# A recurrent layer with interleaved input products: groups of two steps in place of three, and an aligned instruction stream on TensorE

## The chip, the cores and the metric

One core of a Trainium2 chip runs the kernel. The metric is the device time of one execution, in microseconds (us). For the kernel before there are nine executions, with a median of 3041.02 us (3037.76 to 3044.69). A difference below 0.2%, some 6 us, is about what a measurement of this kernel can't tell from no change.

## What is computed

There are N = 64 sequences of T = 256 steps with D = 1024 features. Layer 0 is a plain recurrent network whose result is added to its input; layer 1 scales by a gate that doesn't depend on the step:

```python
xW = jnp.einsum('ntd,dh->nth', x, Wx) + b
next_h = jnp.tanh(prev_h @ Wh + xw)          # 256 times, one after the other
x = x + h_t
h = jax.nn.silu(q_pool @ W1.T + b1)
gate = jax.nn.sigmoid(h @ W2.T + b2)
# Haar levels of v, each times gate, put together again; then x + (v + that)
```

A Haar transform that is multiplied by one gate at all levels and undone is a multiplication by that gate, so layer 1 is a factor of 2 + gate for each sequence and feature. All in float32.

## The kernel before, in words

Two kinds of work take turns on TensorE.

**Steps of h.** `h @ Wh` for one step is done by Strassen's method: seven products (`strassen_product`, L192) in place of eight. A product is 16 calls of `nc.tensor.matmul` (L197), each 32 rows by 128 columns on a quarter of the array. Plain float32 takes two passes, so that each call becomes two weight loads and two matmuls on the chip: 64 instructions a product, 448 a step, 224 of them matmuls. The order in a step is product 1, 4, 2, 5, 6, 7, 3, so that what the next step needs first is ready first; `tanh` (L756), the transposes (L760) and the additions (L780 to L806) run on ScalarE and VectorE beside the next products. The input part `xw` of a step reaches the accumulators by a copy on ScalarE before the products (`put_part`, L611 to L614).

**Pairs of x.** `x @ Wx` is computed for a pair of two steps at once (`S = 2`), in three parts for precision, by `XWork.whole` (L333): 48 matmuls of 128x512 (L276) in a one-pass format, each with one weight load, 96 instructions. They go to the banks `mixed` and `main`. ScalarE takes `mixed` (L321), GpSimd adds the bias (L322), VectorE adds `main` (L376), and the sum goes to DRAM (`store`, L384) and comes back in the layout of the steps (`reload`, L388, eight DMAs).

The first 12 steps (0 to 11, `ALONE = 12`) are handled by another loop (L508), with half a pair beside each step. From step 12 on the loop at L743 runs **groups** of steps; the order on every engine and on SP, which issues the transfers, is the program's own (the schedule is manual). `groups` (L632) holds their lengths: 80 groups of `M = 3`, and 4 steps at the end. After each group `beside_x` (L654) fills the gap with pairs of x: it stores the sum of the pair that was computed last (`later`), not before `mark`, the copy of product 6 in the last step (L794), loads the x of a later pair (`load_next`), issues the reload, and computes the pair `coming` with `now.whole()` (L666). If that pair is needed within the next group, it is stored and reloaded at once, and a second pair follows in the same gap (`many`, L665, L701 to L704). Since a group of three takes one and a half pairs, gaps of one pair and of two alternate. In the gap VectorE adds h to x for the last step (`residual`), GpSimd multiplies by the factor (`scale`), finished pairs are stored to y (`store_done`), ScalarE puts the first accumulators of the next group (after `take_mixed`), and `kept_step` handles an early step that had been set aside, one action a gap.

The sum of a pair, its split parts (`x1`, `x2`) and the high bits have one buffer each; the tiles `xw` have four in turn; the x of pairs has six.

## Time and profile before

| what | value |
|---|---|
| median of nine executions | 3041.02 us |
| the profiled execution's own time | 3044.69 us |
| its span, first to last instruction | 3042.8 us |
| outside the span | 1.9 us |
| VectorE, ScalarE, GpSimd busy | 59%, 28%, 25% |
| data queue, share of 16 DMA engines | 28.1% |
| granted TensorE clock | 1.00 |

The profiled execution is the slowest of the nine. The page gives busy time by engine, the chain of work that ended last, and groups of equal instructions; matmuls are pipelined and their ends are modelled, so that TensorE counts as busy for nearly all of the span whether or not it is fed at its best rate. What it really takes is read from the start of one stretch to the start of the next. "issue" is time for which the profile shows no other engine or transfer as the cause. The trace records the start of every weight load and matmul, of the semaphore waits on the engine's sequencer, and of every DMA packet, those that bring instructions among them.

### The profile page before, as it was taken

What the parts mean: (1) busy time and instruction counts of PE and PEld (TensorE: products, weight loads), DVE (VectorE), ACT (ScalarE), POOL (GpSimd) and SP (SyncE); (2) the same over time, 40 slices, a digit from 0 to 9 for tenths busy, and PEclk for the clock granted to TensorE, in tenths of its full rate; (3) what the DMA queues carried; (4) which work ended last, traced back from release to release, by engine and by line L of the source; (5) the groups of instructions that cost most, each with busy time, mean ns of one, the idle gap of its engine ahead of it and who ended that gap; (6) DMA issues with size and microseconds to landing.
All of it is one profiled execution on the core that took longest, in us unless ns stands there. A gap on an engine that the chain in (4) does not pass through costs nothing.

```text
span 3042.8 us, 141755 instructions
## 1 busy us (share of the span) xinstructions
PE 3030.9 (100%) x63862; PEld 2716.0 (89%) x63862; DVE 1802.2 (59%) x4928; ACT 863.6 (28%) x2641; POOL 775.1 (25%) x521
## 2 busy tenths in 40 slices
PE   9999999999999999999999999999999999999999
PEld 6888999988889998999988889989899988888998
DVE  7555555655556656556655555556555655555555
ACT  3222222222222222222222223222222222222222
POOL 2223222232222222222222222222222222222221
PEclk9999999999999999999999999999999999999999
DMA  7323222333322222222222322222222222322222
GB/s 264 119 100 103 93 93 93 109 103 104 111 94 86 86 97 94 93 86 86 93 99 99 104 89 86 86 86 100 98 86 86 86 100 99 107 92 86 86 86 83
DMA packets 164605, 300.40 MB, mean 99 GB/s; under 512 B 44192, under 2 KB 110496, under 8 KB 164000
## 3 DMA queue, kind: packets, MB, share of 16 engines
q1 hardware_dynamic: 163856, 290.81, 28.1%
q8 instruction: 501, 8.21, 1.1%
q14 instruction: 104, 0.85, 0.1%
q10 hardware_dynamic: 144, 0.52, 0.1%
HBM read 154.93 MB, written 136.31 MB: 96 GB/s over the span
## 4 chain that ended last, share of the span: by engine, by line
PE 98%; DMA 1%; POOL 0%; issue 0%; DVE 0%; SPq 0%; DVEq 0%; ACT 0%
PE main L276 30%; PE acc L197 22%; PE mixed L276 16%; PE m_h L197 14%; PE main_h L197 14%; PE m L197 1%; DMA wh<-wh 0%; DMA h0T<-condT 0%; DMA w<-w1T 0%; PE gate_ps L214 0%; POOL sum L322 0%; DMA x<-xT 0%; DMA b_row<-b 0%; DVE x L300 0%; SPq L132 0%
## 5 line engine op out<-in xcount | busy, mean ns | idle before, releaser
L276 PE MATMUL main<-wx,x 128*128 128x512 f32 x4064 | 945.8, 389 | 0.2 <-DVE x L300 0.2
L276 PEld LDWEIGHTS main<-wx,x 128*128 128x128 f32 x4064 | 762.1, 188 | 161.0 <-issue 2.6
L501 POOL TENSOR_TENSOR x<-x,factor 128x512 f32<-128x512 f32 x242 | 312.4, 1291 | 1316.6 <-DVE x L619 933.3
L322 POOL TENSOR_TENSOR sum<-sum,b_row 128x512 f32<-128x512 f32 x254 | 423.5, 1677 | 835.0 <-ACT sum L321 783.6
L276 PE MATMUL mixed<-wx,x 128*128 128x512 f32 x2032 | 494.0, 395 | 0.0
L276 PEld LDWEIGHTS mixed<-wx,x 128*128 128x128 f32 x2032 | 374.9, 188 | 92.1 <-issue 16.9
L756 ACT ACTIVATE h<-h 128x128 f32<-128x128 f32 x976 | 275.7, 306 | 561.2 <-DVE h L780 373.8
L300 DVE TENSOR_TENSOR x<-x,x_high 128x1024 fp32r<-128x1024 f32 x127 | 180.5, 1421 | 261.6 <-PE main L276 261.6
L760 DVE STREAM_TRANSPOSE hT<-h 128x128 f32<-128x128 f32 x972 | 297.8, 306 | 38.3 <-ACT h L756 38.2
L376 DVE SCALAR_TENSOR_TENSOR sum<-main,sum 128x512 f32<-128x512 f32 x254 | 175.4, 691 | 199.6 <-PE main L276 175.7
L197 PE MATMUL acc<-wh,s 128*32 128x128 f32 x8160 | 278.7, 273 | 1.0 <-issue 0.9
L197 PE MATMUL acc<-t,hT 128*32 128x128 f32 x8160 | 273.1, 273 | 2.3 <-issue 2.2
L197 PE MATMUL acc<-wh,hT 128*32 128x128 f32 x8160 | 273.9, 273 | 0.5 <-issue 0.5
L197 PE MATMUL m_h<-t,s 128*32 128x128 f32 x7808 | 266.2, 273 | 0.5 <-issue 0.3
L197 PE MATMUL main_h<-wh,s 128*32 128x128 f32 x7808 | 265.7, 273 | 0.6 <-issue 0.5
L197 PE MATMUL main_h<-t,s 128*32 128x128 f32 x7808 | 264.2, 273 | 0.2
L197 PE MATMUL m_h<-wh,hT 128*32 128x128 f32 x7808 | 262.1, 274 | 0.1
L305 DVE SCALAR_TENSOR_TENSOR x<-x_high,x 128x1024 fp32r<-128x1024 f32 x127 | 182.6, 1438 | 132.4 <-PE mixed L276 132.3
L321 ACT ACTIVATE sum<-mixed 128x512 f32<-128x512 f32 x254 | 146.9, 598 | 362.9 <-DMA sum_d<-sum 192.5
L197 PEld LDWEIGHTS m_h<-wh,hT 128*32 128x32 f32 x7808 | 213.0, 110 | 29.4 <-issue 29.2
L197 PEld LDWEIGHTS acc<-wh,s 128*32 128x32 f32 x8160 | 234.7, 110 | 3.1 <-issue 3.1
L197 PEld LDWEIGHTS acc<-wh,hT 128*32 128x32 f32 x8160 | 230.8, 110 | 3.2 <-issue 1.8
(81 smaller groups left out, 2740.2 us busy)
## 6 DMA issues: line engine op xcount, KB each, us to landing
x<-xT SPq DMA_DIRECT2D x127, 512.0 KB, 4.6
sum_d<-sum SPq DMA_DIRECT2D x127, 512.0 KB, 2.9
xw<-sum_d SPq DMA_DIRECT2D x1016, 64.0 KB, 2.0
yT<-x SPq DMA_DIRECT2D x122, 512.0 KB, 2.8
wh<-wh SPq DMA_DIRECT2D x8, 512.0 KB, 10.8
w<-w1T SPq DMA_DIRECT2D x8, 512.0 KB, 8.5
w<-w2T SPq DMA_DIRECT2D x8, 512.0 KB, 4.3
wx<-wx SPq DMA_DIRECT2D x7, 512.0 KB, 8.6
```

The lines of the kernel that those rows point to most:

```text
L197: nc.tensor.matmul(out=out[q * R : (q + 1) * R], lhsT=a[:, k * R : (k + 1) * R], rhs=wh_s.sides[i][k][:, q], start=first and k == 0, stop= ...
L276: nc.tensor.matmul(out=acc[h], lhsT=v[:, k * P : (k + 1) * P], rhs=wx_s[k][which][:, h * HALF : (h + 1) * HALF], start=start and k == 0, s ...
L300: nc.vector.tensor_sub(self.x1, x, self.high)
L305: nc.vector.scalar_tensor_tensor(out=self.x2, in0=self.high, scalar=1.0 + DOWN, in1=pairs[i], op0=ALU.mult, op1=ALU.subtract)
L321: nc.scalar.activation(s, self.mixed[h], AF.Copy, scale=-1.0)
L322: nc.gpsimd.tensor_add(s, s, b_row[:, h * HALF : (h + 1) * HALF])
L376: nc.vector.scalar_tensor_tensor(out=v, in0=self.main[h], scalar=1.0 + DOWN, in1=v, op0=ALU.mult, op1=ALU.add)
L501: nc.gpsimd.tensor_mul(of_step(x, s), of_step(x, s), blocks(factor))
L756: nc.scalar.activation(quad(h, j), quad(h, j), AF.Tanh)
L760: nc.vector.transpose(quad(hT, j), quad(h, j))
```

## The change

`M` becomes 2. `groups` becomes 120 groups of two steps and 4 steps at the end. A group of two needs one pair, so that the test for a second pair is never met: each of the 121 gaps (one ahead of the first group, and one after each group of two) holds one pair. The pair that a group needs is the one computed in the gap before the last, and it is stored and reloaded in the gap just ahead of the group.

In each pair, ahead of the last two matmuls (`h == 1 and k == B - 2`), `nc.tensor.addr_align(256)` is issued, when `whole` is not followed by a second pair. The built program holds 121 such instructions, with an alignment of 256 instructions, no offset, and up to 255 no-ops as filler.

```diff
-M = 3
+M = 2
...
+BLOCK = 256
...
-        def whole(self) -> None:
+        def whole(self, aligned: bool = False) -> None:
...
             for h in range(2):
                 for k in range(B):
+                    if aligned and h == 1 and k == B - 2:
+                        nc.tensor.addr_align(BLOCK)
                     x_matmul(self.main, self.x0, 0, h, k, stop=True)
...
-    groups = [M] * ((T - ALONE) // M - 1) + [(T - ALONE) % M + M]
+    groups = [M] * ((T - ALONE) // M - 2) + [(T - ALONE) % M + 2 * M]
...
-        now.whole()
+        now.whole(not many)
```

The built programs have as many instructions on VectorE, ScalarE, GpSimd and the DMA queues as before; on TensorE's sequencer there are 631 semaphore waits in place of 671.

## The prediction

> **What bounds the kernel now.** I read the page first: who is busy, and whose chain ends last.

> ```profile
> span 3042.8 us, 141755 instructions
> PE 3030.9 (100%) x63862; PEld 2716.0 (89%) x63862; DVE 1802.2 (59%) x4928; ACT 863.6 (28%) x2641; POOL 775.1 (25%) x521
> ...
> q8 instruction: 501, 8.21, 1.1%
> ...
> PE 98%; DMA 1%; POOL 0%; issue 0%; DVE 0%; SPq 0%; DVEq 0%; ACT 0%
> ```

> TensorE's stream is the chain; nothing else is near. But "busy" hides slow feeding, so the second view is the chain of waits over one gap of two pairs and the group behind it (start us, us, what):

> ```profile
> 957.72 3.85 PE mixed L276 x16
> 961.57 7.25 PE main L276 x32
> 968.82 3.63 PE mixed L276 x16
> 972.45 7.25 PE main L276 x32
> 979.70 1.01 PE m_h L197 x32
> 980.71 1.75 PE acc L197 x64
> ```

> A pair behind steps of h takes 3.85 + 7.25 us, a pair behind a pair 3.63 + 7.25: entering x costs 0.22 us. The first product of h after x takes 1.01 us where two products take 1.75: returning costs 0.14 us. The third view is the sums over whole stretches (us, busy by engine): a clean group of three, a gap of one pair, a gap of two, and another group of three.

> ```profile
> 909.59:928.07 18.48, 18.48 (x673) 18.28 (x673) 11.64 (x44) 6.73 (x24) 2.59 (x2) 1.00 0.04 15
> 928.07:939.17 11.10, 11.10 (x52) 8.93 (x49) 6.58 (x13) 2.17 (x7) 4.77 (x3) 1.00 0.52 173
> 957.65:979.63 21.98, 21.98 (x100) 17.95 (x97) 11.71 (x18) 4.31 (x10) 8.11 (x5) 1.00 0.54 184
> 626.48:646.58 20.10, 19.41 (x673) 18.40 (x673) 11.94 (x44) 6.82 (x24) 2.69 (x3) 1.00 0.10 34
> ```

> The same 672 matmuls took 18.48 us once and 20.10 us another time. The chain inside the slow group says where:

> ```profile
> 640.32 1.74 PE acc L197 x62
> 642.06 0.23 issue
> 642.28 0.30 PE acc L197
> ...
> 645.31 0.67 PE acc L197 x26
> 645.98 0.27 issue
> 646.24 0.41 PE acc L197 x3
> ```

> These are breaks that no engine or data transfer ended. From the starts of all matmuls in the trace, 39 of the 80 groups of three take 18.477 us to within 1 ns, and the other 41 lose between 0.02 and 1.63 us: 16.0 us in all. I numbered TensorE's instructions in program order (two weight loads and two matmuls for a plain float32 call, one of each for x, and the semaphore waits). In most of these groups the first late matmul, 0.1 us or more behind a clean group's, stands at 193 to 195 modulo 256. Row q8 gives the reason: 501 packets of 8.21 MB, 16,384 bytes each, for TensorE's 128,398 records, so 256 instructions a packet. The stalls are **instruction blocks that arrive late**. They are almost all in the third step: no group has lost anything at the end of its first step, the sum is 1.2 us at the end of the second and 16.0 us at the end of the third. Leaving x, the sequencer is well ahead of the array (a matmul of x takes 227 ns, one of h 27.3); in h that lead is used up, and nothing rebuilds it before the next gap.

> [...]

> **The change part by part.** The sum is made in the profiled execution (3044.69 us, span 3042.8).

> *Transitions.* A clean group of three is 18.477 us. Its third step, start to start, is 6.113, so a clean group of two is 12.364. A gap of one pair is 11.108 (mean of 41, from 11.101 to 11.146); gaps of two average 21.987.
> Before: 80 x 18.477 + 455.4 (41 gaps of one) + 879.5 (40 gaps of two) = 2813.1, and 16.0 of stalls: 2829.1 us.
> After: 120 x 12.364 + 121 x 11.108 = 2827.8 us, without stalls.
> So 40 more round trips between h and x cost **+14.7 us**. Nothing hides them: they are the array's own stream, and their size does not vary with the stalls or with the length of the gap ahead.

> *Stalls taken away.* **-16.0 us**, since there is no third step. What remains is the stall of first and second steps. From below it is zero. From above, by the mean of all 80 groups at the end of the second step, 1.2 us / 80 x 120 = 1.8 us. The alignment decides where in that interval: it starts a block four instructions ahead of h, so blocks end near matmuls 126, 254 and 382 of a group's 448. Fifteen groups of before have boundaries within some 10 matmuls of these places, and together they lost 0.04 us in two steps: 0.3 us for 120. I take **+0.4 us**. The third boundary also lies ahead of the mark (behind product 6 of the second step, matmul 384), from which the pair's store starts, so data traffic does not meet that fetch at its start.

> *The no-ops.* A cycle has 2 x 448 + 96 + 5 semaphore waits = 997 instructions, so 27 no-ops fill it to 1024, four blocks. No row shows a no-op. The nearest rows are the sequencer's own semaphore waits, 51 ns each in the trace: 27 x 51 = 1.4 us a gap. The cover is the queue of x matmuls: the stream had lost nothing at the end of any first step, so the sequencer enters h with a full lead, which it can only have gained during x. Below: nothing. Above: 120 x 1.4 = 165 us, bare. The 40 semaphore waits that go could give 2 us if they were bare, and they are as well covered. I take 0 for both.

> *Work that moves to a shorter gap.* Every gap now has what only the two-pair gaps had: the reload must land and ScalarE must put the first accumulators before h resumes, in 11.1 us and not 22.

> ```profile
> 956.33 0.34 SPq L386 DMA_DIRECT2D sum_d<-sum  x1
> 956.76 0.39 SPq L119 DMA_DIRECT2D x<-xT  x1
> 961.19 3.62 SPq L399 DMA_DIRECT2D xw<-sum_d  x8
> ```

> ```profile
> 964.56 0.67 ACT L614 COPY acc<-xw 128x128 f32<-128x128 f32 x3 [2.21 <-DMA xw<-sum_d]
> ```

> This gap began at 957.65. The store leaves ahead of it, the reload waits on SP for the store's landing, and the put ends at 965.2, 7.6 us in. Over all 40 gaps of two the last put ends 2.1 to 7.8 us in. So 3.3 us remain of 11.1 at worst: cost 0, and beyond that 1 us per us and gap. Behind the reload on SP stands only the y store; behind the put on ScalarE only the copy for h. DVE is busy 6.6 of 11.1 us in a gap of one, GpSimd 4.8. One store, one load, eight reloads and one y store a pair are the same counts as before; the queued early steps (one action a gap) only finish sooner.

> *The end.* The last four steps exist in both. Before, they hold 2.4 us of stalls, with the last pair's store and two y stores beside them. The same transfers stand there after; I take the same, between 0 and twice that.

> **Sum**: +14.7 - 16.0 + 0.4 = **-0.9 us**, 3044.69 - 0.9 = 3043.8 us in terms of the profiled execution. That one is the slowest of nine, 3.67 us above the median. The stalls are the part of the chain that varies from one group to the next with no change of work. If the median execution simply has 3.67 us less of them, the change takes less away from it, and its own time stays at 3043.8. If the difference lies elsewhere, it becomes 3041.02 - 0.9 = 3040.1. I hold the first for twice as likely and forecast **3042.5 us**: no change that can be told. Own range 3038 to 3047.

> **The rivals.**

> *The no-ops are not covered (slower).* If they pass through the array's queue at the rate of h (27.3 ns for two instructions), 27 x 13.65 = 0.37 us x 120 = 44 us, 3087 us; bare on the sequencer 165 us, 3209 us. It decides from the point at which the sequencer is less than 1.4 us ahead when it meets them. For: no no-op is in the trace. Against: 227 ns a matmul in x leaves the sequencer idle most of the time. Chance 0.08.

> *The stalls come back (slower).* The fixed places may suit badly, for instance because each short gap leaves fetches behind data traffic (DMA share 0.52 in a gap, 0.04 in a clean group). At the 0.2 us that a group of three lost on average: 24 us, 3067 us. Against: fifteen groups with the same places. Chance 0.07, with smaller forms of it inside the forecast's range.

> *The alignment does nothing.* Then the mean over all places holds, 1.8 us of stalls in place of 0.4: 3043.9 us from the forecast, within its range. It is part of its chance.

> *Transitions shrink (faster).* If entering x is slow because the sequencer arrives late from the third step, groups of two would save 0.23 us in each of 121 gaps, 28 us: 3015 us. Against: gaps behind stalled and clean groups take the same 11.10 us. Chance 0.10, with partial gains.

> **How the numbers follow.** Forecast 0.75, slower rivals 0.15, faster 0.10. The range, 3036 to 3050, is the forecast's own with a few us towards partial forms of the rivals on both sides.

> **What would show it.** Groups of two at 12.36 us nearly without exception; 121 gaps near 11.11 us; about 514 instruction packets (27 x 120 more instructions); puts ending before 8 us in a gap; the mean step unchanged at 6.11. It would be wrong if gaps took over 11.2 us (no-ops or late puts), if groups lost more than 0.05 us on average, or if gaps fell under 11 us.

## The result, and the profile after

The changed kernel takes **3056.13 us** (median of nine, 3054.71 to 3057.66), the kernel before 3040.37 (29 executions, 3034.79 to 3045.45). The ratio is 1.0051, with a 95% interval of 1.0043 to 1.0060: slower by half a per cent, where no change was forecast. The profiled execution took 3057.18 us.

The page answers the questions of the prediction's first view:

```profile
span 3055.4 us, 144905 instructions
PE 3035.7 (99%) x63862; PEld 2708.7 (89%) x63862; DVE 1799.0 (59%) x4928; ACT 871.1 (29%) x2641; POOL 843.7 (28%) x521
...
q8 instruction: 514, 8.42, 1.1%
...
PE 98%; DMA 1%; issue 0%; POOL 0%; DVE 0%; SPq 0%; DVEq 0%; ACT 0%
```

TensorE is still the chain, there are 13 more instruction blocks as counted, but its busy share is 99% and no longer 100%. The waits of TensorE (line waited for: us in total, times, longest) say that this is one break; the second row had 3.6 us in ten waits before:

```profile
PE main L277 <- issue: 10.1, 1, 10.1
PE acc L198 <- issue: 2.7, 4, 1.1
```

10.1 us, once. The chain shows where (start us, us, what): in the very first gap, ahead of the last two matmuls of the pair, which is where the alignment stands.

```profile
186.54 6.80 PE main L277 x30
193.34 10.11 issue
203.45 1.19 PE main L277 x2
204.65 1.86 PE m_h L198 x32
206.51 2.48 PE acc L198 x64
```

The products of h behind it also take 1.86 and 2.48 us in place of 1.01 and 1.75. The sums over stretches show why. The first column is the length in us; then follow the busy time of TensorE, its weight loads, VectorE, ScalarE and GpSimd, the granted clock, the DMA share and GB/s. In order: the first gap, a later gap, the first group, and the time from 197.63 us on for which the clock was lowered.

```profile
182.58:204.58 22.00, 11.89 (x53) 9.06 (x49) 7.62 (x11) 3.26 (x7) 6.34 (x3) 0.84 0.12 40
429.73:440.83 11.10, 11.10 (x52) 8.93 (x48) 6.59 (x13) 2.27 (x7) 5.16 (x3) 1.00 0.57 173
204.58:218.52 13.94, 13.94 (x449) 13.44 (x449) 7.18 (x27) 4.45 (x15) 1.28 (x1) 0.88 0.05 17
...
197.63:207.87 10.24, 4.42 (x66) 3.50 (x70) 0.69 (x1) 1.21 (x2) 0.00 (x0) 0.50 0.01 2
```

Later gaps take 11.10 us, and later groups 12.36 by the starts of their matmuls, as forecast. The first gap takes 22.00: 10.9 too many. From 197.63 us, inside its break, the clock is at one half for 10.24 us; the last 4.4 of them lie behind the break and make the first group 1.58 us longer. Together 12.5 us.

What stands in that break is on record too: line 346, the alignment, has its own entry among the sources (engine, operation, count, duration of one, first and last start).

```profile
L346 PEldq NOP  x3437: 13/13/13, 189.1 to 3020.6; - x191
```

3437 no-ops are 120 x 27 + **197**. The trace has 197 in the first gap, from 189.12 to 203.38 us, 73 ns apart (14.3 us), though each record lasts only 13. In every other gap there are 27, over 1.9 us. What stands ahead of the first alignment is the whole first part of the program and no cycle of 997 instructions, so its filler is whatever is left to the next block. The late matmuls of the kernel before stood at 193 to 195 modulo 256 by my count, so I take it that some 62 instructions are loaded ahead of the kernel's own. With them, the count of TensorE's instructions to that place is 59 modulo 256, and 256 - 59 = 197. (The runs below that work out their offsets from this 59 got the number of no-ops that they asked for, 37 in their first gap.) The no-ops begin 4.06 us before the array is through with the matmuls queued ahead of them, there as in each of the other 120 gaps; the other 10.2 us are the break.

### The profile page after: what moved, and what is told of

It is laid out like the page before. It is cut to its first block, busy times and chain, and to the rows that moved or that the text cites. A ratio compares the mean times of both kernels' runs of the same rounds, so it can differ in the third digit from the quotient of the medians.

```text
span 3055.4 us, 144905 instructions
## 1 busy us (share of the span) xinstructions
PE 3035.7 (99%) x63862; PEld 2708.7 (89%) x63862; DVE 1799.0 (59%) x4928; ACT 871.1 (29%) x2641; POOL 843.7 (28%) x521
## 3 DMA queue, kind: packets, MB, share of 16 engines
q1 hardware_dynamic: 163856, 290.81, 27.3%
## 4 chain that ended last, share of the span: by engine, by line
PE 98%; DMA 1%; issue 0%; POOL 0%; DVE 0%; SPq 0%; DVEq 0%; ACT 0%
PE main L277 30%; PE acc L198 22%; PE mixed L277 16%; PE m_h L198 15%; PE main_h L198 14%; PE m L198 1%; DMA h0T<-condT 0%; DMA wh<-wh 0%; DMA w<-w1T 0%; PE gate_ps L215 0%; POOL sum L323 0%; DMA x<-xT 0%; DMA b_row<-b 0%; DVE x L301 0%; SPq L133 0%
## 5 line engine op out<-in xcount | busy, mean ns | idle before, releaser
L277 PE MATMUL main<-wx,x 128*128 128x512 f32 x4064 | 946.5, 389 | 10.3 <-issue 10.1
L504 POOL TENSOR_TENSOR x<-x,factor 128x512 f32<-128x512 f32 x242 | 358.6, 1482 | 2042.4 <-issue 1177.1
L277 PEld LDWEIGHTS main<-wx,x 128*128 128x128 f32 x4064 | 762.3, 188 | 171.4 <-issue 12.7
L323 POOL TENSOR_TENSOR sum<-sum,b_row 128x512 f32<-128x512 f32 x254 | 447.2, 1781 | 50.6 <-DMA w<-w1T 43.8
L301 DVE TENSOR_TENSOR x<-x,x_high 128x1024 fp32r<-128x1024 f32 x127 | 171.1, 1347 | 253.5 <-PE main L277 253.5
L777 ACT COPY y<-m_h 128x128 f32<-128x128 f32 x244 | 65.0, 266 | 779.1 <-PE m_h L198 763.9
L198 PE MATMUL acc<-wh,s 128*32 128x128 f32 x8160 | 271.4, 273 | 0.4 <-issue 0.4
L198 PE MATMUL m_h<-t,s 128*32 128x128 f32 x7808 | 259.6, 273 | 0.0
L198 PE MATMUL main_h<-wh,s 128*32 128x128 f32 x7808 | 259.5, 273 | 0.0
L306 DVE SCALAR_TENSOR_TENSOR x<-x_high,x 128x1024 fp32r<-128x1024 f32 x127 | 191.9, 1511 | 86.9 <-PE mixed L277 86.8
L783 DVE TENSOR_TENSOR h<-acc,y 128x128 f32<-128x128 f32 x244 | 71.2, 292 | 280.8 <-PE acc L198 280.8
```

What stands on the lines that cost most here:

```text
L198: nc.tensor.matmul(out=out[q * R : (q + 1) * R], lhsT=a[:, k * R : (k + 1) * R], rhs=wh_s.sides[i][k][:, q], start=first and k == 0, stop= ...
L277: nc.tensor.matmul(out=acc[h], lhsT=v[:, k * P : (k + 1) * P], rhs=wx_s[k][which][:, h * HALF : (h + 1) * HALF], start=start and k == 0, s ...
L301: nc.vector.tensor_sub(self.x1, x, self.high)
L306: nc.vector.scalar_tensor_tensor(out=self.x2, in0=self.high, scalar=1.0 + DOWN, in1=pairs[i], op0=ALU.mult, op1=ALU.subtract)
L323: nc.gpsimd.tensor_add(s, s, b_row[:, h * HALF : (h + 1) * HALF])
L504: nc.gpsimd.tensor_mul(of_step(x, s), of_step(x, s), blocks(factor))
```

## The experiments

Theory A: the first alignment's no-ops made the loss, and 53 or so are free. Rivals: the first gap, now of one pair, was too short for its work; the no-ops or the transitions cost something everywhere; the lost time in groups is chance. Each run was measured beside the kernel before, whose median went from 3038.56 to 3041.11 us between them, so that ratios are the better measure between runs. "The groups lose" always means: in the run's one profiled execution, against clean groups of 18.477 us (three steps), 12.364 (two) or 24.590 (four).

**The first filler spread over 17 gaps.**

```diff
+STEPS = [96 + 10 * g for g in range(16)]
...
-                        nc.tensor.addr_align(BLOCK)
+                        nc.tensor.addr_align(BLOCK, offset=STEPS.pop(0) if STEPS else 0)
```

> The changed kernel, but with the 197 no-ops of its first alignment spread: the first 17 gaps get 37 no-ops each, by offsets that grow by 10 a gap, and end at the same block positions; the other gaps keep 27. Theory A (the first alignment meets an instruction position that needs 197 no-ops, at 73 ns each 14.3 us, of which some 4.0 are covered by queued matmuls; then the clock is halved for 10.2 us): the 10.3 us break, 0.7 us in the last two matmuls and 1.6 us in the first group go, and the median falls by 12 to 13 us, to 3042.5 to 3045. The first gap takes 11.1 us. Theory B (the first gap is slow because the work of that gap, now of one pair and not of two, is late: a transfer or an engine): the gap stays at 20 us or more, and the time at 3056. Theory C (transitions cost more than the trace says, and the first gap is a side show): the time falls by less than 6 us.

Measured: 3045.52 us, 10.6 below the changed kernel; against the kernel before, 1.0024 (1.0014 to 1.0033). No gap in its trace is over 11.15 us, the longest group is 12.64, and the chain at the same place has no break:

```profile
184.56 7.25 PE main L278 x32
191.81 1.01 PE m_h L199 x32
192.82 1.75 PE acc L199 x64
```

Theory A holds. The two profiled executions differ by 12.7 us, as expected. The medians fall by less than the 12 to 13 us expected: 10.6 us, or some 8 by the ratios (1.0051 and 1.0024). More on that below. Theory B falls: the same gap with the same work takes 11.1 us.

**Groups of two without alignment.**

```diff
-        now.whole(not many)
+        now.whole()
```

> Groups of two without any alignment. Theory A: no no-ops, so no break in the first gap, 121 gaps of 11.10 to 11.15 us; stalls of 1 to 4 us in the groups of two, since blocks end anywhere; the median at 3043 to 3047, that is 0.1 to 0.2% above the kernel before, and 9 to 13 us below the changed one. Theory B (a gap of one pair at the start is too short for its work): the first gap stays at about 22 us and the time near 3056. If alignment matters as much as the change supposes, this one is slower than the spread alignment by more than 2 us; I expect 0 to 3.

Measured: 3044.43 us, ratio 1.0019 (1.0010 to 1.0027). Gaps of 11.08 to 11.15 us; the groups lose 5.8 us in all, with 2.1 where the positions are held. Against the spread kernel that is 1.1 us faster by the medians, within their intervals, where 0 to 3 us slower were expected: for groups of two the alignment is worth nothing that can be measured. In the profiled executions the last four steps take back part of what the groups give: they lose 3.1 us in the spread kernel and 0.5 here.

**The alignment alone, on groups of three** (`M = 3` and `groups` as before, the rest of the change kept).

> The alignment alone: groups of three as before, with the change's alignment, which then stands in the gaps of one pair. By count of instructions the first alignment needs 189 no-ops and the other 40 need 80 to 88. Theory A (73 ns a no-op, 4.0 us covered): the first costs 9.8 us and a clock drop, each of the others 80 x 0.073 - 4.0 = 1.8 us, 40 of them 74 us; stalls in the groups fall by some 8 us because h then starts at slots 4 and 11 of a block; 3040 + 10 + 2 + 74 - 8 = 3118, between 3105 and 3135. Rival (no-ops are free, and what cost time in the changed kernel is the first gap's own work): 3027 to 3035, since the stalls of the third step go and no transition is added.

Measured: 3129.33 us, ratio 1.0299 (1.0285 to 1.0313), as theory A had it. TensorE's waits:

```profile
PE main L277 <- issue: 74.2, 41, 9.6
```

41 breaks: 9.6 us in the first gap that has an alignment, 1.6 on average in the other 40 (39 with 80 no-ops, the last with 88). The part on the groups missed: they lose 15.0 us, no less than before. By exact count they start at slots 5 and 14 of a block. The 39 at slot 14 behind full gaps of two pairs lose 0.7 us together, the 40 at slot 5, right behind the uncovered no-ops, 14.0, 0.03 us each behind the first end of a block already. That fits a lead that such a gap leaves used up, but nothing else tests it.

**A sweep of the number of no-ops**, which grows by eight every eight gaps:

```diff
+PADS = [37] + [27 + 8 * (g // 8) for g in range(120)]
+PLACE = [59]
...
-                        nc.tensor.addr_align(BLOCK)
+                        PLACE[0] += PADS.pop(0)
+                        nc.tensor.addr_align(BLOCK, offset=PLACE[0] % BLOCK)
+                        PLACE[0] += 997
```

> A measurement of the no-ops by themselves: groups of two, with 37 no-ops in the first gap, then 27, 35, 43 and so on to 139, eight gaps each. Theory A: a gap takes 11.10 us up to about 55 no-ops, then 11.10 + 0.073 x n - 4.0 us: 12.2 at 75, 13.9 at 99, 16.9 at 139; sum over the 120 gaps about 280 us, so 3320 us in all, with a little more where a long break halves the clock. Rival (a no-op costs nothing, or the cost is one of the first gap only): all gaps at 11.1, 3044 us. Rival (no-ops are covered by the whole 11 us of x): all gaps at 11.1 as well.

Measured: 3461.3 us, one execution. The sums over one gap each with 51, 59, 99 and 139 no-ops:

```profile
840.28:851.38 11.10, 11.10 (x53) 8.93 (x49) 6.58 (x13) 2.27 (x7) 5.16 (x3) 1.00 0.53 172
1029.32:1040.85 11.53, 11.36 (x53) 8.86 (x49) 6.57 (x13) 2.27 (x7) 5.16 (x3) 1.00 0.48 166
...
2072.36:2087.00 14.64, 11.58 (x53) 8.85 (x49) 6.60 (x13) 2.28 (x7) 5.15 (x3) 0.98 0.38 131
3282.21:3300.05 17.84, 11.85 (x53) 9.06 (x49) 6.60 (x13) 2.29 (x7) 5.16 (x3) 0.95 0.32 109
```

The first column behind the stretch is its length. From 27 to 51 no-ops a gap stays at 11.10 us, at 59 it is 11.5, and from there on every eight cost 0.6 (12.7 on average at 75): 74 ns each, starting at some 55, which is the 4.06 us by which the sequencer is ahead. (The expectation's 12.2, 13.9 and 16.9 us are 0.4 below its own formula.) The gaps gain 318 us, where 284 follow from 0.073 us a no-op and 4.0 us of cover. At 59 to 75 no-ops, with the clock at 1.00, a gap takes some 0.1 us more than that sum. The rest of the miss goes with the clock, 0.98 and 0.95 in the last two rows: from 83 no-ops on (a break of 2.0 us or more) it is halved for 3.4 or 6.8 us at 60 of the 64 breaks, and the groups there take 13.5 to 14.6 us on average in place of 12.36. All groups together lose another 102 us.

**The kernel before with nothing but one alignment in its first gap** (199 no-ops):

```diff
-                now.whole()
+                now.whole((None, 99 if mark is None else None))
```

The line is that of the second pair in the gap. Here and below `whole` takes two offsets, for an alignment ahead of matmul 16 and of matmul 46 of the pair, or None for no alignment.

> The kernel before with one alignment only, ahead of the last two matmuls of the first gap: by count 199 no-ops, and none anywhere else. It has no other part of the change. Theory A (the first alignment is what made the changed kernel slow): +10.4 us in that gap, +0.6 in its last two matmuls, +1.6 us in the group behind it at half clock, so 3051 to 3055 against 3039 to 3041 of the kernel before; the blocks of all later groups are shifted as well, so some us of stalls more or less. Rival (it needs the single pair in the first gap): no difference.

Measured: 3052.23 us, ratio 1.0042 (1.0026 to 1.0057). The chain at the end of that gap, now one of two pairs:

```profile
202.64 10.53 issue
213.17 1.19 PE main L276 x2
214.36 1.87 PE m_h L197 x32
```

The same break with the full work of two pairs ahead of it, and without groups of two: the loss belongs to the no-ops alone. The profiled execution, 3047.22 us, is 5 us below the median of its four; its later groups, whose positions are shifted, lose 8.0 us and not 16.0.

**Groups of three at held block positions.** 40 no-ops in each of two places of a gap of one pair, 144 in four places of the first gap:

```diff
-        now.whole()
+        now.whole(FIRST if mark is None else (None, None) if many else (s - 105, s - 4))
```

`FIRST` stands for the offsets of the first gap, whose second pair has two of its own. With s = 40, groups start at slots 41 and 50 of a block, and for the opposite, s = 200, at 201 and 210.

> Groups of three as in the kernel before, with block positions held: 80 no-ops in each gap of one pair, in two places of 40 (ahead of matmul 16 and of matmul 46), which the 53 no-ops that a place covers should hide, and 144 in four places of the first gap. Every group then starts at slot 41 or 50 of a block, where the groups of before lost little. Theory A (no-ops below 53 a place are free, and what a group of three loses depends on where blocks end): gaps of one pair stay at 11.10 us, the groups lose under 5 us in all, and the median is 5 to 9 us below the kernel before, 3030 to 3035. Rival (stalls are chance, whatever the position): 10 to 16 us of stalls, no difference from before. Rival (two places do not each have their own cover): gaps of one pair at about 13 us, 75 us slower.

Measured: 3039.97 us, ratio 0.9999 (0.9991 to 1.0008). The no-ops were covered (gaps of 11.10 to 11.15 us), but the groups lose 10.0 us, not under 5: the expectation missed, my choice of the position was a poor one.

> The same with every group at slot 201 or 210, where the groups of before lost most (0.6 to 0.75 us on average over nine groups). No-ops as in the other in the gaps of one pair, 48 in the first gap. Theory A: 80 groups lose 0.5 to 0.8 us each, 40 to 60 us in all, so 25 to 50 us above the kernel before, 3065 to 3090. Rival (position does not matter): within 5 us of the kernel with slots 41 and 50.

Measured: 3066.34 us, ratio 1.0086 (1.0072 to 1.0100); the groups lose 39.4 us. With as many no-ops in the gaps of one pair, only the position differs by 160 slots. A group there, in the chain of waits:

```profile
1737.60 0.11 issue
1737.71 0.31 PE acc L197 x4
...
1741.41 0.68 issue
1742.09 0.43 PE acc L197 x8
```

The breaks of 0.11 and 0.68 us lie at the fifth and sixth end of a block in the group (matmuls 539 and 667 of 672).

**Groups of four, unaligned** (`M = 4` in the kernel before).

> The other direction: groups of four, without alignment, so 61 gaps of two pairs and 61 groups. By the prices of transitions (0.14 + 0.23 us) 19.5 round trips less, -7 us. If the lead of the sequencer is used up by the third step, the fourth loses as much again or more: the third lost 14.8 us over 80 groups, 0.18 each, so the fourth 0.2 to 0.4 us over 60 groups, and the third 0.18: some 23 to 35 us of stalls in place of 10 to 16. In all 3 to 15 us above the kernel before. Rival (stalls happen once for a group, not once for a step): 11 us of stalls, 3030 to 3034.

Measured: 3046.28 us, ratio 1.0013 (1.0004 to 1.0022). In the profiled execution 60 groups lose 21.2 us, 0.35 each, against 0.20 for a group of three. That is 5 us more in all, and less than the 7 us of transitions saved; that execution, 3041.15 us, is 5 us below the median of its ten. The median is above the kernel before all the same. Whether the other executions lose more in their groups is not shown.

**Groups of three at slots 2 and 11, and at 20 and 29** (s = 1 and s = 19).

> The kernel with groups of three and held block positions, now at slots 2 (behind a gap of one pair) and 11 (behind a gap of two). No-ops as there, 40 a place. With slots 41 and 50 the 80 groups lost 9.9 us, with 201 and 210 39.4; with the change's own alignment on groups of three the 39 groups at slot 11 lost 0.7 us together, but 40 at slot 4, behind uncovered no-ops, 14.0. If position alone decides, 80 groups lose 2 to 5 us here, and the time is 5 to 9 us below the kernel before, 3030 to 3035. If the gap ahead decides (one pair: bad, two pairs: good), the groups behind one pair lose 0.2 to 0.35 us each again and the time is that of the kernel before within 4 us.

Measured: 3033.22 us, ratio 0.9979 (0.9970 to 0.9988). The groups lose 3.6 us; those behind one pair 0.046 each, those behind two 0.043. So whether the gap ahead holds one pair or two doesn't decide.

> The same at slots 20 and 29. If position decides smoothly, between the ones at 2/11 and 41/50: 3 to 10 us of stalls, 0 to 8 us below the kernel before.

Measured: 3032.26 us, ratio 0.9983 (0.9975 to 0.9992). The groups lose 2.5 us, less than at either neighbour and than the 3 to 10 expected; 66 of the 80 take the clean 18.48 us. Three groups in a row, from the sums over stretches, one of them clean and two of the other 14:

```profile
1675.30:1693.78 18.48, 18.48 (x674) 18.28 (x673) 11.65 (x44) 6.73 (x24) 2.59 (x2) 1.00 0.04 15
1704.88:1723.54 18.66, 18.66 (x673) 18.41 (x673) 11.68 (x44) 6.75 (x24) 2.57 (x2) 1.00 0.05 17
1745.57:1764.14 18.57, 18.57 (x673) 18.27 (x673) 11.57 (x43) 6.64 (x24) 2.59 (x2) 1.00 0.05 17
```

These two beat both kernels: the alignment is worth 5 to 6 us on groups of three, if its filler is covered and the position is right. That is about the smallest difference that these measurements can tell. Their last four steps lose 3.7 us (slots 2 and 11) and 4.2, where the kernel before loses 2.3.

**The kernel before once more.**

> The kernel before, unchanged, for a second profile of it: what its stalls are in an execution nearer to the median. If what varies from one execution to the next is the stalls alone, this one's time less its stalls in groups of three is 3044.7 - 16.0 = 3028.7 within 2 us: an execution of 3040 us has 10 to 13 us of them. If the rest varies, the stalls stay at 16 us at any time.

Measured: 3044.18 us, with 16.0 us lost in its groups again. The difference, 3028.1, agrees with the first profile's 3028.7, but this execution is not near the median either, so it can't settle what the median executions lose.

The mean loss of a group just behind each end of a block, from the starts of its matmuls (us, summed up to there; groups of three are the 40 behind gaps of one pair):

| kernel, slot of the group's start | ends at matmul | behind the 1st, 2nd, ... end |
|---|---|---|
| groups of three, 201 | 27, 155, 283, 411, 539, 667 | 0.00, 0.00, 0.04, 0.08, 0.28, 0.62 |
| groups of three, 41 | 107, 235, 363, 491, 619 | 0.00, 0.00, 0.00, 0.05, 0.09 |
| groups of three, 20 | 118, 246, 374, 502, 630 | 0.00, 0.00, 0.00, 0.01, 0.03 |
| groups of two, plain, four ends | at any four | 0.00, 0.02, 0.04, 0.07 |
| groups of two, plain, three ends | at any three | 0.00, 0.00, 0.01 |

So the loss goes by the ends of blocks within a group, not by the step: the first two or three cost next to nothing, and behind them the loss grows from end to end. The number of ends alone is not the rule. A group of three has five ends, or six if it starts at slot 192 or later. In the two profiles of the kernel before, counted in the same way, the 14 groups at slots 193 to 209 lose 0.70 us on average, the 22 at slots 216 to 255, with six ends as well, 0.05, and the 124 with five ends 0.17. Nor is the position all: those groups of before that start at slots 1 to 24 lose 0.12 us on average, the held ones at 2 to 29 lose 0.04.

The instruction packets in the traces show a slip. At slot 201 the first packet behind the array's passing of a block's end starts 0.62 us after it at the first end and 1.48 us at the fifth (medians of the 40 groups behind gaps of one pair); at slot 41 it is 0.30 and 1.13 us, at slot 20 it is 0.23 and 0.78. The packets start latest where most is lost. What sets their start, and why 41 costs some four times as much as 20, stays open.

## Why the prediction was wrong, step by step

- **The step that failed is the no-ops**: "27 no-ops fill it to 1024 ... I take 0". True of 120 gaps, by the sweep with a wide margin (27 of some 55). But I worked out the filler for the cycle, and the first alignment is not behind a cycle. It needed 197, of which some 55 are covered: 10.2 us of break, 0.6 in the two matmuls at half clock, 1.6 in the group. The rival "not covered" had this very mechanism, with its point of decision ("less than 1.4 us ahead") for 27 no-ops in all gaps and a price of 44 to 165 us; I did not ask whether all gaps had as many. Its bare price, 51 ns a no-op after the record of a semaphore wait, was too low as well: the no-ops start 73 ns apart.
- **Transitions, +14.7 us: right.** 112 of the 120 groups take 12.364 us within 0.02, and every gap but the first 11.10 to 11.15.
- **Stalls, -16.0 + 0.4 us: right in the profiled executions.** The 120 groups lose 2.7 us, of which 1.6 is the first one at half clock; 1.1 remain, where 0.4 were taken, between 0 and 1.8. The spread kernel's profiled execution, 3044.45 us, stands 0.24 below the profiled 3044.69 of before; the sum said 0.9 below.
- **The relation to the median failed by some 5 us.** The spread kernel is 1.0024 of the kernel before, 7 us; its profiled execution lies 1 us below its median, while the two profiled ones of the kernel before lie 4 to 5.5 us above theirs. I had held for likely that a median execution of before simply loses less in its groups, 12.3 us; about 10 would fit (14.7 + 2 less 7 us). An execution without a profile can't be looked into, so this stays argued. It made 3042.5 about 3 us too low, within the stated range; without the first filler the forecast would have held.
- **Work in a shorter gap, 0: right.** All gaps but the first take 11.10 to 11.15 us. The last four steps lose 2.5 us where they lost 2.3, as was taken.
- **What the stalls are: right in kind, too narrow in cause.** They are late blocks, but not a matter of the third step: 26 us lie between two positions of the same groups of three (3039.97 and 3066.34). That h uses up the sequencer's lead, and that nothing rebuilds it, was my estimate; no run measured the lead inside h. What the traces show there is that the instruction packets start later behind the array at the fifth end of a block than at the first (1.48 and 0.62 us at slot 201). Had I read the groups of before by the slot of their start as well, and not by the step alone, the spread from 0.05 to 0.70 us would have been in sight, and with it the better change: hold the position and keep the groups of three.

## What to carry to other kernels

A filler that is free in a loop's steady cycle has a first time: work out its length for the first place too, where what lies ahead is another count. Ask of any padding how far the sequencer is ahead at that point (here 4.06 us, 55 no-ops at 74 ns), and split it over several places if it is longer (two places of 40 were covered here, with gaps of 11.10 to 11.15 us; 80 in one place broke the stream for some 1.6 us). Held at slots 20 and 29, groups of three lost 0.03 us each (2.5 us in 80), less than the 0.05 of the shorter groups of two at positions that were not held (5.8 us in 120). Choose the position by measurement: the positions held here at 2 to 29 and those at 201 and 210 lie more than 1% apart in one and the same kernel, some 31 to 33 us (0.9979 and 0.9983 of the kernel before against 1.0086).
